# Attention start of a Mamba, mixture-of-experts and attention kernel: first tile gathered in one row, key inputs fetched earlier, keys and ternary pieces redistributed

## The chip, the cores and the metric

The kernel runs on one core of one Trainium2 chip, in one launch. A core has TensorE (PE, with its weight loads shown apart as PEld), VectorE (DVE), ScalarE (ACT), GpSimd (POOL) and SyncE (SP), each with its own instruction queue that is worked off in order, and DMA engines that move data between memory and the core. The metric is the device time of the launch in microseconds (us), as a median of several runs. One more run was recorded with the profiler; all views of the trace are of that run.

## The reference

The input x is [4, 512, 512] (2048 tokens of width 512, 16 tiles of 128 tokens), the context is [4, 512, 256]. Four residual blocks follow each other:

```python
x = x + _L0_xattn_ref(ctx_1024, _layernorm(x, axis=-1), ...)   # selective state-space scan
x = x + _L0_ffn_ref(_layernorm(x, axis=-1), ...)               # 64 experts, top 8, rerouted
x = x + _L1_xattn_ref(_layernorm(x, axis=-1), ctx_1024, ...)   # 16 heads, RMS-normed q and k
x = x + _L1_ffn_ref(x, L1_ffn_w1, L1_ffn_w2)                   # two ternary "bitlinear" layers
```

Three things of it matter here. The experts' results are weighted and added, eight for each token:

```python
y = lax.ragged_dot(hact, jnp.swapaxes(down_proj, 1, 2), group_sizes)
w = top_val.reshape(-1)[order]
out = jnp.zeros_like(x).at[tok].add(y * w[:, None])
```

The attention's keys depend on the context alone, so they can be made at any time before they are read, one task for each of 4 batches and 16 heads:

```python
k = (encoder_hidden_states @ Wk).reshape(B, Skv, H, D)
k = rmsnorm(k, gk)
```

And both weights of the last block are turned into ternary numbers by the mean of their absolute values, which needs two passes over each:

```python
scale = 1.0 / jnp.clip(jnp.mean(jnp.abs(w)), EPS, None)
return jnp.clip(jnp.round(w * scale), -1, 1) / scale
```

## The kernel before

The kernel has stages that follow each other on the same core: the state-space scan (`ssm_phase`, up to about 583 us of the span), the routing (`route`, to about 702), the experts (`Experts.run_in`, to about 1467), a conditional that handles tokens beyond the room of an expert (`tc.If(many > 0)` in `moe_phase`), and the attention with the last feed-forward (`attend`). Inside `ssm_phase`, `route`, `run_in` and `attend` the order of the instructions on each engine is that in which the Python code calls them (`manual_schedule`).

*Keys.* The class `Keys` makes one key at a time in four steps: `task` (two matmuls of PE, pk, L1091), `evict` (ACT squares pk into k_sq and copies it scaled into k_kT, L1100 and L1101, and SP stores k_kT to k_dram), `squares` (PE sums the squares into kpss, L1111) and `take` (ACT takes kpss into k_ms, L1123). Keys are made in three places: beside the scan, in the experts (`key_tasks`, one for each expert until the list is empty) and at the start of the attention (`KEYS_LATE`: heads 8 to 15 of batches 2 and 3, 16 keys). For these last ones two contexts (k_ctx, L2039) and the weights (k_w, L1082) are loaded when the attention begins. `last_keys` turns their mean squares into inverse roots (`rsqrt`, an ACT table load, a square root and five DVE operations), transposes them on PE (pkr, L2092) and stores them to r_dram.

*Experts.* Iteration i of `run_in` gathers the rows and weights of expert i + 2 (POOL's indirect DMAs xg, wg, wd), multiplies gate and up of expert i - 1 (pg, L1191) between the transposes of expert i's rows, runs a key task, and multiplies down for expert i - 2 (po, L1215 and L1225). The rows are stored to y_dram by SP (L1237). Between pg and the next matmuls lie ACT's `sg`, DVE's `h` (L1198, L1200) and ACT's copy of half of `h` (L1202). After each expert a share of a task list is worked off:

```python
while tasks and done < (i - 1) * many / E:
    tasks.pop(0)()
```

The list has 44 tasks that find each token's rows and weights, then the ternary tasks (`Ternary.tasks`: load a piece wf of 1 MB, L1634 and L1636; reduce its absolute values, L1649; a mean over partitions by PE, L1656; and in a second pass scale, clip and round it, L1664 to L1666), then the norms of all earlier keys (`key_norms`: a load of ms_dram, an rsqrt, and PE transposes kpt, L1463).

*Attention's start.* For batch 0 the eight expert rows of each token are gathered from y_dram by POOL (yg, L1132, one 128 x 512 piece for each of 4 tiles x 8 slots, in four buffers) and added into x_all by DVE (L1722). When a tile is complete, its statistics (L1728 on DVE; ve_c, L1732, and rstd_c, L1734, on POOL), its normed form xn_c, its transpose (pt, L1747) and the queries of head groups 0 and 1 (pq, L1790; norms qms and rq on POOL, L1801 and L1802; qn, L1808; transpose pqt, L1817) follow, and the first scores (psc, L1824). All of this is put into a list with due times in an imagined clock, and the list is called in order of these times:

```python
GAP, FLIGHT = 1.25, 3.5
for n in range(NC * TOPK):
    later(n * GAP, fetch, 1)
    later(n * GAP + FLIGHT, add, 1)
...
for i, (b, h) in enumerate(KEYS_LATE):
    later(5 + 2.7 * i, some_keys, b, h)
```

The times set only the order of the calls; an engine that has its inputs does not wait for them. `norm_k` (POOL multiplies kT by its inverse norm rk, L1782) of heads 0 to 2 stands at the times 4, 6 and 8. Before the list, SP is given the loads of k_ctx, k_w, Wq and the first three heads' kT, rk and v.

*Attention's loop.* It runs over units u, four for each of 64 heads: scores for unit u, values (po, L1851) once a head, the transposes (pet, L1844) of unit u - 2, then what `front[u]` and `back[u]` hold. `put` enters work there: queries of the next head group, projections (px, L1860) of the group before, gathers and the feed-forward of earlier batches. In the first four heads no queries and no projections are entered.

Of the kernel before, what the change touches and what calls it, by code (L numbers as in the profile page):

```python
# [731 lines left out]
def moe_phase(ctx, cm, x_all, w, kv, dr, out):  # L732
# [14 lines left out]
    tern = Ternary(cm, keep, w)  # L747
    with ExitStack() as es:
# [3 lines left out]
        with tc.manual_schedule(), tc.tile_pool(name="e_w", bufs=4) as wp:  # L752
            ex = Experts(cm, w, dr, y_dram, r, wp)
            route(cm, x_all, w, kv, dr, r, more, keys, ex)
            ex.run(tern, more, keys, kv)
# [3 lines left out]
    with tc.manual_schedule():  # L759
        attend(cm, x_all, w, kv, y_dram, r["wk"], r["pos"], tern, out)  # L760
# [19 lines left out]
def route(ctx, cm, x_all, w, kv, dr, r, more, keys, ex):  # L780
# [19 lines left out]
    def iota(shape, name, pattern, mult=0, dtype=I32):  # L800
        t = cp.tile(shape, dtype, name=name)
        gp.iota(t, pattern=pattern, base=0, channel_multiplier=mult)
        return t
# [17 lines left out]
    def made(name, shape, pattern, mult=0, dtype=F32):  # L821

        t = iota(shape, f"{name}_i", pattern, mult)
        plan.at(plan.now + 5, cast, t, name, dtype)
# [31 lines left out]
    mT = cp.tile([E, NT, P], F16, name="mT")  # L856
# [383 lines left out]
class Experts:  # L1240
# [18 lines left out]
    def run(self, tern, more, keys, kv):  # L1259
        with ExitStack() as es:  # L1260
            self.run_in(es, tern, more, keys, kv)

    def run_in(self, ctx, tern, more, keys, kv):
# [9 lines left out]
        key_list = key_tasks(keys, self.w, kp, ex.ps)  # L1273
# [3 lines left out]
        done = 0  # L1277
        self.load_rows(0)
        self.load_rows(1)
        for i in range(E + 2):  # L1280
# [10 lines left out]
            if i >= 2:  # L1291
                ends = list(range(ROWS[i - 2], ROWS[i - 1], P)) + [ROWS[i - 1]]
                ex.down(st[i - 2], [self.y_dram[r0:r1, :] for r0, r1 in zip(ends, ends[1:])])
                while tasks and done < (i - 1) * many / E:
                    tasks.pop(0)()
                    done += 1
            keys.squares()
        assert not tasks and not key_list


def key_tasks(keys, w, pool, ps):

    nc = keys.nc
    left = [(1, h) for h in range(3, H)] + [(b, h) for b in (2, 3) for h in (6, 7)]
# [5 lines left out]
    def load(b0, h0, b, h):  # L1310

        if b != b0:
            t = ctx[b] = pool.tile([P, CTX // P, S], F32, name="k_ctx")
            nc.sync.dma_start(t, w["ctxT"][:, b * S:(b + 1) * S].rearrange("(k p) s -> p k s",
                                                                           p=P))
        if h // HG != h0 // HG:
            keys.load(h // HG * HG, (h // HG + 1) * HG, pool, "k_w")

    def task(n):
        keys.task(*left[n])  # L1320
        keys.evict()
        if n + 1 < len(left):
            load(*left[n], *left[n + 1])

    load(-1, -1, *left[0])
    return [lambda n=n: task(n) for n in range(len(left))]
# [290 lines left out]
class Ternary:  # L1617
    def __init__(self, cm, keep, w):
# [4 lines left out]
        self.part = [keep.tile([P, NC], F32, name=f"part{n}") for n in (1, 2)]  # L1623
        self.ws = [keep.tile([P, 1], F32, name=f"ws{n}") for n in (1, 2)]

    def tasks(self, pool, ps):

        cm, nc = self.cm, self.cm.nc

        def load(n, c):  # L1630
            t = pool.tile([P, DH], F32, name="wf")
            src = self.w[f"w{n + 1}T"].rearrange("(c p) o -> c p o", p=P)
            if n == 0:
                nc.sync.dma_start(t, src[c])  # L1634
            else:
                nc.sync.dma_start(t.rearrange("p (k o) -> p k o", k=NC),  # L1636
                                  src[c * NC:(c + 1) * NC].rearrange("k p o -> p k o"))
            return t

        loads = [(n, c) for n in range(2) for _ in range(2) for c in range(NC)]  # L1640
# [6 lines left out]
        def add(n, c):  # L1647
            fetch()
            nc.vector.tensor_reduce(self.part[n][:, c:c + 1], ready.pop(0), AX.X, ALU.add,  # L1649
                                    apply_absolute_value=True)  # L1650

# [8 lines left out]
        def round_(n, c):  # L1660
            fetch()
# [4 lines left out]
            nc.scalar.activation(self.out[n][:, c * DH:(c + 1) * DH], t, AF.Copy, bias=-MAGIC)  # L1666

        nc.vector.tensor_copy(self.identb, cm.ident)
        calls = [(fetch,)]
        for n in range(2):  # L1670
            calls += [(add, n, c) for c in range(NC)] + [(mean, n)]
            calls += [(round_, n, c) for c in range(NC)]
# [14 lines left out]
def attend(ctx, cm, x_all, w, kv, y_dram, wk, pos, tern, out):  # L1687
# [26 lines left out]
    def fetch(n):  # L1714
        for _ in range(n):
            t, k = rows.pop(0)
            ygs.append((gather(nc, pool[4], "yg", DM, y_dram[:, :], pos[:, t, k:k + 1]), t, k))
# [193 lines left out]
    def ffn_up(t, half):  # L1911

        if half == 0:
# [3 lines left out]
            hid = pool[1].tile([P, DH], F32, name="hid", tag="eT" if turn else "hid")  # L1917
# [16 lines left out]
    def ffn_h(t):  # L1934
# [4 lines left out]
        hq = pool[2 if turn else 1].tile([P, DH], BF16, name="hq", tag="qT" if turn else "hq")  # L1939
# [7 lines left out]
    def ffn_hT(t, n):  # L1947
        hid, hq, sc, de = ff[t]
        if n == 0:
            ff["hT"] = pool[1].tile([P, NH, P], BF16, name="Th")  # L1950
# [84 lines left out]
    ctx_k = {}  # L2035

    def load_ctx(b, tag):
        t = ctx_k[b] = pool[1].tile([P, CTX // P, S], F32, name="k_ctx", tag=tag)
        nc.sync.dma_start(t, w["ctxT"][:, b * S:(b + 1) * S].rearrange("(k p) s -> p k s", p=P))  # L2039

    keys = Keys(cm, w, kv, small, lambda n: pool[7].tile([P, S], F32, name=f"k_{n}", tag="oT"),
                lambda shape, name: (pav if name == "kpss" else psc).tile(
                    shape, F32, name=name, tag="po" if name == "kpss" else "psc"),
                lambda b: (ctx_k[b], 0), direct=ms)
    first, end = KEYS_LATE[0][1], KEYS_LATE[-1][1] + 1
    load_ctx(2, "hq")
    keys.load(first, end, pool[1], "hid")
    load_q(0)
    load_ctx(3, "Th")
    load_kv(0)  # L2050
    load_q(1)
    load_kv(1)
    load_kv(2)
# [6 lines left out]
    GAP, FLIGHT = 1.25, 3.5  # L2060
    for n in range(NC * TOPK):
        later(n * GAP, fetch, 1)
# [16 lines left out]
    for n in range(3):  # L2079
        later(4 + 2 * n, norm_k, n)  # L2080
    def some_keys(b, h):
        keys.squares()
        keys.task(b, h)
        keys.take()
        keys.evict()

    def last_keys():
        keys.squares()
        keys.take()
        rsqrt(nc, small, ms, ms, "late")  # L2090
        pr = pav.tile([n_ms, P], F32, name="pkr", tag="po")
# [154 lines left out]
```

## Time and profile before

| | |
|---|---|
| median of 3 runs | 2767.82 us (2764.25 to 2768.01) |
| profiled execution | 2769.29 us, of which the span is 2767.4 us |
| mean granted TensorE clock | 0.948 |
| PE busy | 2539.8 us (92%) in 10107 instructions |
| DVE, ACT, POOL busy | 54%, 46%, 43% |
| DMA | 405.21 MB, mean 146 GB/s |
| chain that ended last | PE 41%, DVE 3%, ACT 1%, DMA 1% of the span |

The span reaches from the first to the last instruction. A matmul's end is modelled in the trace, so a busy PE is not PE at its peak. The clock column gives the part of full TensorE speed that was granted. A view by stretches gives the busy time of each engine in each stretch; the waits view says who waited for whom, in total, how many times and the longest; the timeline lists instructions in order of time, with the idle time before them and what ended it in brackets.

### The profile page before, as it was taken

To read this page: it belongs to the slowest core of one execution; us is meant where nothing else is said; L and a number is where in the kernel's file an instruction comes from. 1 tells how busy PE (TensorE), PEld (TensorE's weight loads), DVE (VectorE), ACT (ScalarE), POOL (GpSimd) and SP (SyncE) were. 2 spreads that over 40 slices of the span, in tenths; PEclk is the share of its full clock that TensorE was granted. 3 is DMA by queue.
4 is the path that set the end of the run, shared out by engine and by line. 5 is a ranking of instruction groups with operands and counts; after the bars stand their busy time and mean duration, and the time that the engine had idled before them with its cause. 6 is when DMAs were issued, how large, how long until landed. Compare 5 with 4: busy or idle time off the path is not lost. (4 is left out here: it accounts for less than half of the span.)

```text
span 2767.4 us, 29904 instructions
## 1 busy us (share of the span) xinstructions
PE 2539.8 (92%) x10107; PEld 1436.0 (52%) x10158; DVE 1486.8 (54%) x2546; ACT 1274.1 (46%) x2363; POOL 1181.3 (43%) x1121
## 2 busy tenths in 40 slices
PE   5989897986899999999985989999999999999997
PEld 2545454653456566666663544445555554555543
DVE  5887877966322223333443365545665666544445
ACT  6675757754323322222332443445555554555543
POOL 4888887961333334443433333224431443121212
PEclk8979797987999999999998999999999999999999
DMA  6253535322656656668986344323332443221200
GB/s 243 81 200 102 200 102 188 119 84 80 195 181 209 209 179 220 222 224 306 343 284 209 122 147 131 95 88 126 114 96 80 126 126 99 80 80 51 64 31 19
DMA packets 198352, 405.21 MB, mean 146 GB/s; under 512 B 30372, under 2 KB 71908, under 8 KB 193073
## 3 DMA queue, kind: packets, MB, share of 16 engines
q1 hardware_dynamic: 155566, 249.86, 26.8%
q0 software_dynamic: 40576, 153.19, 17.4%
q8 instruction: 83, 1.36, 0.2%
q14 instruction: 77, 0.62, 0.1%
q10 hardware_dynamic: 2050, 0.18, 0.1%
HBM read 321.22 MB, written 81.92 MB: 146 GB/s over the span
## 5 line engine op out<-in xcount | busy, mean ns | idle before, releaser
L1827 DVE TENSOR_REDUCE mx<-psc 128x1 f32<-128x512 f32 x256 | 176.5, 690 | 452.5 <-PE psc L1824 446.9
L1191 PE MATMUL pg<-xT,wg 128*128 128x284 f32 (+12 forms) x1536 | 399.9, 404 | 14.2 <-ACT h L1202 12.8
L1191 PEld LDWEIGHTS pg<-xT,wg 128*128 128x128 f32 x1536 | 282.6, 194 | 95.1 <-issue 29.7
L1830 ACT ACTIVATE e<-psc,mx 128x512 f32<-128x512 f32 x256 | 176.0, 687 | 320.4 <-DVE mx L1827 320.0
L488 POOL TENSOR_TENSOR dBu<-bb,du 128x1024 f32<-128x1024 f32 x128 | 299.9, 2367 | 26.8 <-DVE dA L511 19.8
L1132 POOL DMA_INDIRECT xg<-xn_dram,tok x168 | 180.7, 1076 | 209.9 <-PE pt L1175 164.7
L1824 PE MATMUL psc<-kT,qT 128*128 128x512 f32 x512 | 264.0, 597 | 1.6 <-ACT qT L1818 1.6
L1851 PE MATMUL po<-eT,v 128*128 128x512 f32 x512 | 235.0, 602 | 10.3 <-ACT eT L1845 10.2
L1790 PE MATMUL pq<-Wq,xnT 128*128 128x512 f32 x512 | 235.0, 603 | 0.7 <-ACT xnT L1749 0.7
L1860 PE MATMUL px<-Wo,oT 128*128 128x512 f32 x512 | 231.5, 595 | 0.0
L511 DVE TENSOR_TENSOR_SCAN dA<-dA,dBu 128x1024 f32<-128x1024 f32 x80 | 183.1, 2289 | 56.9 <-ACT dA L497 46.4
L1801 POOL TENSOR_SCALAR qms<-qms 128x4 f32<-128x4 f32 x64 | 25.5, 398 | 418.1 <-DVE qms L1799 417.2
L1844 PEld LDWEIGHTS pet<-ident,e 128*128 128x128 f32 x1024 | 126.2, 141 | 147.7 <-issue 124.6
L497 ACT ACTIVATE dA<-delta,negA 128x512 f32<-128x512 f32 x256 | 176.5, 692 | 19.0 <-DVE hc L512 12.6
L470 PE MATMUL pv<-Wv,ctxb 128*128 128x512 f32 x256 | 148.1, 709 | 28.7 <-ACT v L476 28.7
L517 PEld LDWEIGHTS yT<-ident,hc 128*128 128x128 f32 x1024 | 130.1, 153 | 83.1 <-issue 57.9
L1851 PEld LDWEIGHTS po<-eT,v 128*128 128x128 f32 x512 | 97.3, 192 | 139.0 <-issue 117.7
L1132 POOL DMA_INDIRECT yg<-y_dram,pos x128 | 128.9, 1007 | 87.5 <-SPq L757 38.5
L1236 DVE COPY yo<-po 128x512 f32<-128x512 f32 x68 | 47.0, 690 | 219.4 <-PE po L1225 219.3
L1844 PE MATMUL pet<-ident,e 128*128 128x128 f32 x1024 | 154.5, 274 | 6.4 <-DVE e L1836 6.4
L517 PE MATMUL yT<-ident,hc 128*128 128x128 f32 x1024 | 145.3, 293 | 11.1 <-POOL hc L512 6.4
L1836 DVE TENSOR_SCALAR e<-e,tot 128x512 f32<-128x512 f32 x256 | 150.5, 588 | 9.1
(352 smaller groups left out, 4384.6 us busy)
## 6 DMA issues: line engine op xcount, KB each, us to landing
y_dram<-yo SPq DMA_DIRECT2D x110, 256.0 KB
bb<-bc_dram SPq DMA_DIRECT2D x16, 1024.0 KB
cb<-bc_dram SPq DMA_DIRECT2D x16, 1024.0 KB
v_dram<-v SPq DMA_DIRECT2D x64, 256.0 KB
k_dram<-k_kT SPq DMA_DIRECT2D x64, 256.0 KB
Wq<-Wq SPq DMA_DIRECT2D x16, 1024.0 KB
kT<-k_dram SPq DMA_DIRECT2D x64, 256.0 KB
rk<-r_dram SPq DMA_DIRECT2D x64, 256.0 KB
```

The lines of the kernel that those rows point to most:

```text
L488: nc.gpsimd.tensor_tensor(dBus[q], st[b]["bb"][i // 2][:, j:j + 2, :], st[b]["du"][c].unsqueeze(1).to_broadcast([P, 2, S]), ALU.mult)
L497: nc.scalar.activation(dAs[q][:, j, :], st[b]["delta"][c], AF.Exp, scale=negA[:, c, n:n + 1])
L511: nc.vector.tensor_tensor_scan(*flat, 0.0, ALU.mult, ALU.add)
L517: nc.tensor.matmul(yT[:, lc, :], t[:, lc * P:(lc + 1) * P], cm.ident, is_transpose=True, start=first and lc == 0, stop=last, skip_group_ch ...
L1132: nc.gpsimd.indirect_dma_start(out=t[0:n, :], out_offset=None, in_=table, in_offset=bass.IndirectOffsetOnAxis(ap=index, axis=0))
L1191: nc.tensor.matmul(pg[:, 0:n], s["wg"][:, c, m * P:(m + 1) * P], s["xT"][:, c, 0:n], start=c == 0, stop=c == NC - 1)
L1790: nc.tensor.matmul(pq.rearrange("p h d -> p (h d)"), xnTs[b * NC + i][:, c, :], s["Wq"][:, c, :], start=c == 0, stop=c == NC - 1)
L1824: nc.tensor.matmul(pscore, st[b, g]["qT"][:, h, i * P:(i + 1) * P], ks[n], start=True, stop=True)
L1827: nc.vector.tensor_reduce(mx, pscore, AX.X, ALU.max, negate=True)
L1844: nc.tensor.transpose(pt[:, kc, :], e[:, kc * P:(kc + 1) * P], cm.ident)
L1851: nc.tensor.matmul(po, v[:, kc, :], eT[:, kc, :], start=kc == 0, stop=kc == KB - 1)
L1860: nc.tensor.matmul(px, oTs[j * HG + h][:, i * P:(i + 1) * P], st[b, g]["Wo"][:, h, :], start=h == 0, stop=h == HG - 1)
```

## The change

Four things are changed.

1. A pool `late` is opened around the experts and the attention. It holds the tiles named hid, hq and Th, which the attention used for key weights, contexts and the last feed-forward, and in which the routing now also keeps two of its constants. The key tasks of the experts load their inputs there, in a new order (batches 2 and 3 first, then batch 1), with weights for eight heads at a time. After the last of them the context of batch 2 is loaded again, so that contexts and weights of the 16 last keys are in place when the attention begins.
2. The 16 last keys are split: the eight of batch 2 stay in the start (times 0, 2.6, ... 15.6 and 22), the eight of batch 3 are put into the loop, one each head, at the fourth unit of heads 1 to 8. `last_keys` moves into the loop at unit 40.
3. The second four of the first tile's gathers go into a tile yg_first of their own, and `norm_k` and the loads of heads 1 and 2 get later times.
4. Ternary pieces are half as large (4 KB a partition, 512 KB), two loads are asked for ahead, each new load follows the use of a piece, and the whole task list is worked off by the 54th expert.

The diff, cut to these parts:

```diff
@@ moe_phase
+    late = ctx.enter_context(tc.tile_pool(name="b_late", bufs=1))
...
-            ex.run(tern, more, keys, kv)
+            ctx_k = ex.run(tern, more, late, keys, kv)
...
-        attend(cm, x_all, w, kv, y_dram, r["wk"], r["pos"], tern, out)
+        attend(cm, x_all, w, kv, y_dram, r["wk"], r["pos"], tern, late, ctx_k, keys.wk, out)
@@ route
-        t = cp.tile(shape, dtype, name=name)
+        t = late.tile(shape, dtype, name=name, tag="hq") if long else cp.tile(shape, dtype, name=name)
...
-    mT = cp.tile([E, NT, P], F16, name="mT")
+    mT = late.tile([E, NT, P], F16, name="mT", tag="Th")
@@ Experts.run_in
+        QUOTA = 54
...
-                while tasks and done < (i - 1) * many / E:
+                while tasks and done < (i - 1) * many / QUOTA:
@@ key_tasks
-    left = [(1, h) for h in range(3, H)] + [(b, h) for b in (2, 3) for h in (6, 7)]
+    left = [(b, h) for b in (2, 3) for h in (6, 7)] + [(1, h) for h in range(3, H)]
+    late_b = KEYS_LATE[0][0]
...
-            t = ctx[b] = pool.tile([P, CTX // P, S], F32, name="k_ctx")
+            t = ctx[b] = late.tile([P, CTX // P, S], F32, name="k_ctx",
+                                   tag="hq" if b > late_b else "Th")
...
-        if h // HG != h0 // HG:
-            keys.load(h // HG * HG, (h // HG + 1) * HG, pool, "k_w")
+        if h // (2 * HG) != h0 // (2 * HG):
+            h0 = h // (2 * HG) * 2 * HG
+            keys.load(h0, h0 + 2 * HG, late, "hid")
...
+        else:
+            load(*left[n], late_b, KEYS_LATE[0][1])
@@ Ternary.tasks
+        L = NC * DH // (2 * NC)
...
-        loads = [(n, c) for n in range(2) for _ in range(2) for c in range(NC)]
+        loads = [(n, c) for n in range(2) for _ in range(2) for c in range(2 * NC)]
...
         def add(n, c):
-            fetch()
             nc.vector.tensor_reduce(self.part[n][:, c:c + 1], ready.pop(0), AX.X, ALU.add,
                                     apply_absolute_value=True)
+            fetch()
...
         def round_(n, c):
-            fetch()
             t = ready.pop(0)
...
-            nc.scalar.activation(self.out[n][:, c * DH:(c + 1) * DH], t, AF.Copy, bias=-MAGIC)
+            nc.scalar.activation(self.out[n][:, c * L:(c + 1) * L], t, AF.Copy, bias=-MAGIC)
+            fetch()
...
-        calls = [(fetch,)]
+        calls = [(fetch,), (fetch,)]
@@ attend
-    def fetch(n):
+    def fetch(n, into=None):
         for _ in range(n):
             t, k = rows.pop(0)
-            ygs.append((gather(nc, pool[4], "yg", DM, y_dram[:, :], pos[:, t, k:k + 1]), t, k))
+            yg = pool[4].tile([P, DM], F32, name="yg") if into is None else into
+            nc.gpsimd.indirect_dma_start(
+                out=yg, out_offset=None, in_=y_dram[:, :],
+                in_offset=bass.IndirectOffsetOnAxis(ap=pos[:, t, k:k + 1], axis=0))
+            ygs.append((yg, t, k))
...
-    load_ctx(2, "hq")
-    keys.load(first, end, pool[1], "hid")
+    keys.wk = wk_k
+    first = KEYS_LATE[0][1]
     load_q(0)
-    load_ctx(3, "Th")
     load_kv(0)
-    load_q(1)
-    load_kv(1)
-    load_kv(2)
...
+    wide = pool[1].tile([P, KB, S], F32, name="yg_first", tag="eT")
     for n in range(NC * TOPK):
-        later(n * GAP, fetch, 1)
+        later(n * GAP, fetch, 1, wide[:, n - KB] if KB <= n < 2 * KB else None)
...
-    for n in range(3):
-        later(4 + 2 * n, norm_k, n)
+    for f, n, time in ((load_q, 1, 6), (load_kv, 1, 12), (load_kv, 2, 18),
+                       (norm_k, 0, 20.5), (norm_k, 1, 30.5), (norm_k, 2, 40.5)):
+        later(time, f, n)
...
     def some_keys(b, h):
+        keys.task(b, h)
         keys.squares()
-        keys.task(b, h)
+        keys.evict()
         keys.take()
-        keys.evict()
...
-    for i, (b, h) in enumerate(KEYS_LATE):
-        later(5 + 2.7 * i, some_keys, b, h)
-    later(5 + 2.7 * len(KEYS_LATE), last_keys)
+    for i in range(H // 2):
+        later(2.6 * i if i < 7 else 22, some_keys, *KEYS_LATE[i])
+    later(26, keys.squares)
+    later(26.5, keys.take)
...
+    inside[0] = True
+    for i in range(H // 2):
+        u = KB * (i + 1) + 3
+        put(front, u, keys.task, *KEYS_LATE[H // 2 + i])
+        put(back, u, keys.evict)
+        put(front, u + 1, keys.squares)
+        put(back, u + 1, keys.take)
+    put(back, KB * (H // 2 + 1) + 4, last_keys)
```

In the loop the keys take their PSUM from the pool of the queries and projections (pmm) for pk, and k_sq and k_kT lie in the tiles xn_d and Th. The order of the instructions in the built program differs in two further places, at the edges between stages: at the end of the scan DVE's last `yg`, POOL's last sum into x_all and ACT's last key steps stand ahead of the router's first statistics instead of behind them, and at the end of the experts the last copy of `yo` on ACT and its store to y_dram on SP stand behind the branch of the conditional, where before it was the last store of the key norms.

## The prediction

> **What bounds the kernel now.** I read the page first: TensorE (PE) is busy for 92% of the span and the chain that ended last is PE almost everywhere, so time can be won only where PE waits. The busy time by stage, from the windows view, says where that is.
>
> ```profile
> 1300.00:1400.00 100.00, 93.72 (x427) 66.17 (x426) 44.53 (x61) 30.36 (x56) 46.02 (x44) 1.00 0.99 350
> ...
> 1466.00:1511.00 45.00, 17.21 (x61) 8.28 (x57) 10.94 (x16) 7.92 (x17) 18.23 (x18) 0.75 0.76 257
> 1511.00:1578.00 67.00, 64.21 (x242) 35.88 (x242) 29.10 (x48) 27.42 (x58) 33.38 (x38) 0.96 0.40 126
> 1578.00:1601.00 23.00, 14.66 (x39) 7.14 (x38) 8.66 (x20) 8.60 (x17) 7.66 (x9) 0.78 0.51 163
> 1601.00:1634.00 33.00, 30.33 (x104) 14.78 (x105) 22.98 (x44) 17.49 (x41) 7.50 (x7) 1.00 0.47 148
> 1634.00:1760.00 126.00, 122.86 (x395) 60.37 (x394) 78.21 (x142) 50.89 (x116) 46.98 (x49) 0.99 0.39 122
> ```
>
> Columns: stretch, length, busy PE, PEld, DVE, ACT, POOL, granted clock, DMA share, GB/s. The last experts (1300 to 1400) have the DMA engines full. The attention's start holds 1466 to 1511, where PE works 17.2 of 45 us; 1511 to 1578, where it is full; and a gap before the loop at 1601. From 1634 on PE is full. The waits view names the waits: two rows for the experts, three for the start.
>
> ```profile
> PE pg L1191 <- ACT h L1202: 12.8, 4, 5.0
> ...
> PE pm L1656 <- DVE wone L1654: 3.2, 2, 2.3
> ```
>
> ```profile
> PE pk L1091 <- DMA yg<-y_dram,pos: 14.1, 1, 14.1
> ...
> POOL qms L1801 <- DVE qms L1799: 40.9, 6, 9.8
> ...
> POOL kT L1782 <- DMA v<-v_dram: 12.4, 1, 12.4
> ```
>
> The timeline shows the mechanisms.
>
> ```profile
> 1279.40 2.29 DVE L1649 TENSOR_REDUCE part<-wf 128x1 f32<-128x2048 f32 x1 [9.46 <-DMA wf<-w1T]
> ...
> 1282.97 3.75 PE L1191 MATMUL pg<-xT,wg 128*128 128x256 f32 x8 [4.71 <-ACT h L1202]
> ...
> 1489.39 1.27 POOL L1782 TENSOR_TENSOR kT<-kT,rk 128x512 f32<-128x512 f32 x1 [12.38 <-DMA v<-v_dram]
> ...
> 1506.04 0.69 DVE L1728 BATCH_NORM_STATS2 st_c<-x_all 128x6 f32<-128x512 f32 x1
> ...
> 1581.63 0.39 PE L2092 MATMUL pkr<-ident,k_ms 128*64 128x128 f32 x1 [3.52 <-DVE k_ms L100]
> ...
> 1595.67 1.91 PE L1824 MATMUL psc<-kT,qT 128*128 128x512 f32 x2
> ```
>
> A ternary piece that lands late blocks DVE, with it `h`, and PE stands 4.71 us. At the start POOL's fifth gather stands behind a kT*rk product that waits 12.4 us for loads, so tile 0 is complete only at 1506.04. The chain of waits then runs through keys, each costing PE these two pieces:
>
> ```profile
> 1517.28 0.79 PE kpss L1111 x8
> 1518.07 1.84 PE pk L1091 x4
> ```
>
> that is 2.6 us a key.
>
> **Part 1, the experts.** Removed: the late ternary pieces. A 1 MB piece issued at 1270.8 landed at 1279.4. The four waits on `h` are 12.8 us, of which some 12.7 come from these pieces. After the two long ones the next pg took 3.75 instead of 1.89 (half clock), so 3.6 more: 16.3 us won. The pieces of 512 KB are asked for two ahead, so each has about an expert's period (9 to 10 us), and 84 tasks by the 54th expert spread 16 MB over 24 experts instead of 18.
>
> Here a rule speaks against the change. The Trainium skill ("DMA: Bandwidth & Descriptors", section "Bandwidth") wants at least 1 MiB per DMA, and its section "Anatomy of one DMA" fits 2.0 us plus bytes/436e3. An estimate from that is 4.4 us for 1 MiB and 3.2 for 512 KiB, 16 x 2 = 32 us more transfer time in sum. If pieces stood in series on the path, the 16.3 would be gone and more. The row has 8.6 us for a piece with a second beside it; half of it lands in about 4.5, inside the period. I take the row: nothing added.
>
> Added by the order in which the changed program stands. (a) The key norms: the transpose `kpt` now follows its own rsqrt in one expert's tasks (before, an expert later, with no wait). PE waits for ACT's yo copy 0.59, table load 1.28, sqrt 0.36, DVE 1.35+0.36+0.36+0.26+0.36: 5.3 us with hand-overs, and 1.8 for the half clock. Behind it stand all matmuls of the next expert. (b) Each ternary mean follows the last 1.15 us reduction of its own task group: 2 x 2.3 instead of 3.2, +1.4. (c) Two `remap` tasks in one expert: +1. Together 9.5. Net of part 1: -7 us, between -14 (a to c hidden) and +2 (half the old waits stay).
>
> At nothing: the keys' loads inside the experts. They come an expert ahead, at a DMA share of 0.67 to 0.69 in 1000 to 1200. The 1 MB for heads 8 to 15 is the tight one; uncovered it costs 3 us once. On SP a ternary load now waits for ACT's rounding; behind it stand only the next expert's y_dram stores, an expert later. At the edge of the first stage DVE's last `yg` and POOL's last x_all sum move ahead of the router's statistics, and ACT's k_sq ahead of g_xn. The first g_xn comes 3 us later, but PE's first g_pt (590.31) stood behind a kpss that waited 2.95 for k_ms, which now comes sooner: 0, from -1.5 to +1.5.
>
> **Part 2, the attention's start.** Against it: the last y_dram store moves behind the If on SP (ready at 1471.2). With 0.4 to issue and 1.5 (the r_dram store that stood there) to 3.1 us (y_dram before) to land, the first gather goes from 1472.07 to about 1474. For it: eight gathers 1.25 us apart, in four buffers and the four of yg_first, with nothing between; the eighth is issued near 1483 and lands 3.4 us (the first, before) to 6.3 us (the second, beside loads) later. 2 MB of key inputs are off the queue. Statistics of tile 0, after a ninth add, near 1490 instead of 1506.
>
> Then POOL sets the pace: per tile 8 x 1.25, ve and rstd 0.6 to 1.7, two qms/rq pairs 3.0, one kT product 1.27, so 15 to 16 us. Tile 3's statistics fall near 1537 instead of 1563.1, since 8 keys are gone from PE, 21 us, and some of the others done before. From there to the loop's first psc the trace has 32.6 us: two keys 5.2, last_keys' chain 4.0 (1578.15 to 1582.1), a half-clock pq 2.3 (5.90 for 3.60). Without these 21: 1558 instead of 1595.7, -38.
>
> PE will idle some us in each tile. The Trainium skill ("TensorE: Matmul & The Clock Gate", section "What's actually happening") halves the clock after an idle window of about 3.4 us; by it most gaps here stay free, -38. The row after an idle of 3.57 us paid 2.3 for one pq. I take one or two of those on the path: -35, between -26 (6.3 us landings, 19 us a tile) and -40.
>
> SP's order: Wq of group 1 now stands behind three k_dram stores that wait for ACT, issued near 1482 and needed near 1501; the second and third kT/rk/v loads are needed by POOL some 15 us after issue. At nothing; one that is late costs what it is late, up to the 8.6 us of a loaded 1 MB. The kT product of head 0, moved behind the seventeenth gather, is needed only by the first psc, after tile 1's transposes. The rows that share memory through the new pool (Th, hq, hid) are last read by the routing before the experts begin: nothing.
>
> **Part 3, the loop.** Eight keys come into heads 1 to 8, one each: 8 x 2.6 = 20.9. In heads 1 to 3 PE waits 1.3 us a head, mostly for eT behind the scores; a key fills 0.2 of it: -0.6. ACT's 1.45 us a key fits beside the scores. last_keys' transpose waits there for a table load and five small DVE operations, partly under a 3.4 us projection: +2, from 0 to 4. Sum +22, from +17 to +26.
>
> **Sum.** -7 - 35 + 22 = -20 us: from the profiled execution's 2769.3 (span 2767.4 and 1.9 around it) to 2749.3. The median of the runs shown, 2767.82, lies 1.5 lower: 2748.
>
> **Rivals.** *The start saves less than the loop pays* (slower). If gathers and POOL's chain pace tiles 1 to 3 as slowly as before (20 us a tile), the landings stretch to 6 us and the tail keeps half-clock matmuls, the start gives 10, the experts 7 and the loop takes 22: +5, 2773. It decides once the start saves under 15 us. For it: POOL waited 40.9 us for qms. Against: that qms came late because PE did keys, full for 64 of 67 us. Chance 0.07. *The experts give nothing*: new waits (a to c) and late pieces cancel the 16 us, maybe 5 more: 2755 to 2760. For it: DVE's queue is in order and denser in the first 54 experts. Chance 0.15. *More than I take*: `kpt` partly hidden and the start at -40: 2735. Chance 0.08. The forecast itself: 0.70, 2736 to 2760.
>
> **How the numbers follow.** This kernel's measurement can tell about 0.2% (5.5 us) from no change. Forecast 0.70 and the larger gain 0.08 are faster; of the experts' rival 0.10 is faster and 0.05 the same; of the slower one 0.05 slower and 0.02 the same. So 0.88, 0.07, 0.05. The range, 2732 to 2763, takes in both ends of the start and of the experts, not together.
>
> **What would show it.** Right: no wait on `wf` before 1466 and one new PE wait of about 5 us at `kpt`; the first eleven POOL instructions after the If all gathers; tile 0's statistics 14 to 18 us earlier; first psc of the loop 30 to 40 us earlier, counted from the If; then heads 1 to 8 each 2.3 to 2.6 us longer. Wrong: PE waits on pk or pq in the start for loads, a tile period of 19 us or more, or more than 3 us a key in the loop.

## The result and the profile after

The changed kernel takes 2750.22 us (median of 5 runs, 2747.28 to 2757.41) where the kernel before takes 2768.01 (5 runs, 2764.25 to 2776.38) on the same chip; the ratio is 0.9935, interval [0.9916, 0.9955]. That is 17.8 us faster; 20 were forecast. Its profiled execution took 2754.55 us (span 2752.8), 4.3 more than its median; that of before 2769.29, 1.3 more. In the two profiles the gain is thus 14.6 us, and the stage numbers below add up to that.

Four of the stretches that the prediction read in the windows view, now of the changed kernel (stretch, length, busy PE, PEld, DVE, ACT, POOL, granted clock, DMA share, GB/s):

```profile
1300.00:1400.00 100.00, 91.96 (x410) 65.85 (x409) 36.89 (x65) 34.07 (x64) 40.71 (x41) 0.97 0.84 283
...
1466.00:1511.00 45.00, 33.90 (x113) 17.84 (x112) 17.15 (x27) 12.59 (x27) 24.84 (x27) 0.89 0.82 278
1511.00:1578.00 67.00, 52.68 (x151) 27.52 (x152) 34.01 (x58) 20.39 (x42) 33.15 (x38) 0.82 0.37 111
...
1634.00:1760.00 126.00, 122.27 (x408) 62.32 (x407) 67.81 (x135) 54.69 (x120) 39.74 (x43) 0.99 0.41 128
```

The DMA engines of the last experts are no longer full (0.84 instead of 0.99), yet PE is busy for less of that stretch, so something new stands there. The beginning of the start has twice the PE work, 33.9 us instead of 17.2. Its middle, full before, now has PE waiting and the clock at 0.82. The waits view of PE names both, first for the experts (700 to 1466), then for the start (1466 to 1601):

```profile
PE kpt L1475 <- issue: 5.3, 1, 5.3
...
PE pm L1673 <- DVE part L1665: 3.0, 1, 3.0
...
PE pm L1673 <- DVE wone L1671: 2.2, 1, 2.2
...
PE pg L1194 <- ACT h L1205: 0.4, 1, 0.4
```

```profile
PE pqt L1838 <- DVE qn L1829: 12.0, 4, 3.6
PE pk L1094 <- DVE half L1721: 4.6, 1, 4.6
```

The four waits on `h` are gone (12.8 to 0.4) and the forecast ones are there, `kpt` with just the 5.3 us that were worked out, the two means with 5.2 together. The first `pk` waits 4.6 us instead of 14.1. The timeline of the changed kernel gives the marks of the start:

```profile
1474.47 0.95 POOL L1735 DMA_INDIRECT yg<-y_dram,pos  x1 [33.57 <-issue]
...
1492.22 0.69 DVE L1749 BATCH_NORM_STATS2 st_c<-x_all 128x6 f32<-128x512 f32 x1
...
1543.45 0.69 DVE L1749 BATCH_NORM_STATS2 st_c<-x_all 128x6 f32<-128x512 f32 x1
...
1564.91 1.91 PE L1845 MATMUL psc<-kT,qT 128*128 128x512 f32 x2
```

First gather 1474.47 (1474 forecast), tile 0's statistics 1492.22 (1490), tile 3's 1543.45 (1537), the loop's first psc 1564.91 (1558 to 1561). The tiles are 15.4, 18.1 and 17.8 us apart by their statistics, where the sum had 15 to 16.

To read small terms, the span was cut at four marks: the end of the last `pv` of the first stage to the first `g_pt` (edge); the last `plist` matmul, near the end of the routing, to the last PE matmul ahead of the If (experts); from there to the loop's first psc (start); from there to the end (loop). Two profiles of before exist (the second is run e5), two of the changed kernel (the second is e1).

| us | edge | experts | start | loop | span |
|---|---|---|---|---|---|
| before | 7.3 | 766.8 | 128.8 | 1171.7 | 2767.4 |
| before, e5 | 7.3 | 769.1 | 126.8 | 1168.5 | 2767.5 |
| changed | 10.7 | 764.4 | 97.7 | 1187.9 | 2752.8 |
| changed, e1 | 10.9 | 764.6 | 100.2 | 1185.0 | 2755.3 |

The windows view between these marks shows what a stage consists of; first before, then changed, each as experts, start, loop:

```profile
700.02:1466.83 766.81, 734.82 (x3295) 469.37 (x3294) 252.98 (x448) 217.47 (x470) 304.18 (x293) 0.98 0.71 233
1466.83:1595.67 128.84, 90.33 (x322) 49.04 (x322) 45.68 (x77) 40.92 (x84) 55.28 (x61) 0.86 0.54 177
1595.67:2767.40 1171.73, 1137.45 (x4046) 575.51 (x4096) 663.44 (x1434) 562.25 (x1106) 329.66 (x404) 0.99 0.29 91
```

```profile
702.83:1467.25 764.42, 738.43 (x3295) 471.52 (x3294) 256.70 (x471) 219.27 (x478) 294.31 (x293) 0.97 0.71 232
1467.25:1564.91 97.66, 72.66 (x226) 38.74 (x225) 45.79 (x72) 27.24 (x55) 54.02 (x61) 0.85 0.58 190
1564.91:2752.80 1187.89, 1157.88 (x4194) 589.77 (x4193) 658.75 (x1439) 575.81 (x1134) 329.82 (x404) 0.99 0.29 92
```

Length less busy PE is PE's idle time. A second loss hides in the busy time, the half clock: the same view in steps of 5 us (20 in the loop), length times (1 - granted clock), summed, gives it. The remainder is work at full speed. Experts: idle 32.0 to 26.0, clock 18.8 to 20.4, full-speed work 716 to 718. Start: idle 38.5 to 25.0, clock 17.6 to 14.6, work 72.7 to 58.1. Loop: idle 34.3 to 30.0, clock 10.0 to 9.6, work 1127.5 to 1148.3.

### The profile page after: what moved, and what is told of

It reads as the page before. It is cut to its first block, busy times and chain, and to the rows that moved or that the text cites. A ratio compares the mean times of both kernels' runs of the same rounds, so it can differ in the third digit from the quotient of the medians.

```text
span 2752.8 us, 30001 instructions
## 1 busy us (share of the span) xinstructions
PE 2545.1 (92%) x10158; PEld 1441.3 (52%) x10158; DVE 1486.0 (54%) x2570; ACT 1275.9 (46%) x2371; POOL 1170.6 (43%) x1121
## 5 line engine op out<-in xcount | busy, mean ns | idle before, releaser
L1135 POOL DMA_INDIRECT xg<-xn_dram,tok x168 | 172.2, 1025 | 221.6 <-PE pt L1178 179.2
L497 ACT ACTIVATE dA<-delta,negA 128x512 f32<-128x512 f32 x256 | 176.5, 692 | 18.1 <-DVE hc L512 12.0
L1135 POOL DMA_INDIRECT wd<-down,widx x64 | 63.1, 986 | 216.1 <-PE po L1228 182.2
```

Source lines behind the costliest of these rows:

```text
L497: nc.scalar.activation(dAs[q][:, j, :], st[b]["delta"][c], AF.Exp, scale=negA[:, c, n:n + 1])
L1135: nc.gpsimd.indirect_dma_start(out=t[0:n, :], out_offset=None, in_=table, in_offset=bass.IndirectOffsetOnAxis(ap=index, axis=0))
```

## The experiments

**Yardstick.** No edit.

> The changed kernel once more, on the chip and in the rounds of the next three, as their yardstick. Theory: the stage sums of the first profile come back within 1.5 us each: route entered some 2.8 us later than before, experts 2 us shorter, start 31 us shorter, loop 16 us longer; in sum 14 to 18 us faster than the kernel before. Rival: a stage moves by more from run to run than the effects read from it (over 3 us in one stage), and then none of the small terms may be read from a single profile.

2754.03 us (ratio to before 0.993, [0.9916, 0.9945]). The stages stay within 0.2 us in the experts and within 3 us in start and loop, more than the 1.5 expected and just less than the rival's 3; the entry to the route moved by 2.9 because the first stage's own end moved (its last `pv` at 582.5 and 585.2). So marks are counted from the stage's own beginning below. The runs that follow widen the spread: six profiles with the changed kernel's start (the result, e1, e3, e4, e9, e10) show it at 93.8 to 100.2 us, 96.7 in the mean. A difference under 6 us in the start, or under 3 in the loop, is therefore not read from one profile.

The runs were made on several chips. Times of different chips are compared below by what each gains on the kernel before on its own chip; for the changed kernel that is 17.8 us (the result), 16.7 (e1) and 17.8 (e10).

**The kernel before once more.** No edit.

> The kernel before once more, for a second profile to take stages from. Theory (the small stages move from run to run with the half clock): the experts' full-speed work is 716 us within 1 as in the first profile, the waits on h are again 11 to 14 us, and what differs is the time lost to half clock, by up to 6 us in a stage; the loop lies between 1166 and 1173. Rival: the first profile stands for all, every stage within 1 us.

2768.02 us. Full-speed work in the experts is 717.3 (716.0 before), the loop 1168.5. What differs is idle and clock: the start's lost clock is 22.9 instead of 17.6, the loop's 6.2 instead of 10.0. The theory holds, except that the full-speed work moved by 1.3 where 1 was allowed.

**The ternary part alone, in the kernel before.** The class `Ternary` of the changed kernel, and:

```diff
-                while tasks and done < (i - 1) * many / E:
+                while tasks and done < (i - 1) * many / 54:
```

> The kernel before with the ternary part alone: 512 KB pieces, asked for two ahead, tasks spread over 54 experts. Theory (the new waits cancel most of what the late pieces cost): the four waits on h of 12.8 us go to under 1.5 us, a kpt wait of about 5.3 us and two pm waits of 5.2 us in sum appear, and the experts become 2 to 4 us shorter; start and loop stay within 2 us of before; 2764 to 2767 by the median of before. Rival (pieces cost nothing new and the experts' gain is lost elsewhere in the changed kernel, to the key inputs loaded there): experts 8 to 14 us shorter here.

2760.88 us, ratio 0.9967, [0.9954, 0.998], so 5.5 to 12.7 us faster. The waits come as forecast (`h` 0.7, kpt 5.7, the means 5.2). The experts take 761.5 us: 5.3 and 7.6 below the two profiles of before. That lies between the two expectations. All profiles with this part and the old task order, this one included, show the experts at 764.4 to 764.6 or at 761.1 to 761.5, with 20.4 to 20.5 or 17.0 to 17.1 us of lost clock and 26 to 27 of idle: the two groups differ by what is paid in half clock.

**Each TensorE half of a task one expert later.** A task returns its second half, which the next expert runs first:

```diff
+                todo, halves = halves, []
+                for f in todo:
+                    f()
-                while tasks and done < (i - 1) * many / QUOTA:
-                    tasks.pop(0)()
+                while tasks and not halves and done < (i - 1) * many / QUOTA:
+                    half = tasks.pop(0)()
+                    if half:
+                        halves.append(half)
...
         act.copy(wT, pt)
-        pw = ps.tile([P, NC, E], F32, name="pw", tag="pt")
...
+        def rest():
+            pw = ps.tile([P, NC, E], F32, name="pw", tag="pt")
...
+        return rest
```

(so too in `row` and in the ternary `mean`; step 1 of `key_norms` returns an empty half).

> The changed kernel with each task that ends in a TensorE step cut in two, the TensorE half one expert later: the key norms' kpt after rsqrt, the two ternary means (pm), the four remaps (pw), the two rows (prow). The work is the same. Theory: these waits, 5.3 + 5.2 + 3.5 + 2.0 = 16 us in the changed kernel's profile, all go, and with them most of the half clock that follows them (some 15 us lost between 740 and 1466 by the granted clock): experts 20 to 31 us shorter than in the changed kernel, some 2722 to 2732. Rival (the waits only absorb slack: the next expert's gathers or DVE are late anyway): a wait on xg, h or xT takes their place and the experts become under 8 us shorter.

2728.57 us, ratio 0.9846, [0.9834, 0.9859]: 25.5 below e1. The experts take 738.9 us, 22 to 26 less. The waits on pm, pw and prow are gone and kpt waits for nothing; one new wait of 3.3 us came, pt for the copy `krows` behind the second kpt. Idle 13.3 instead of 26.0, lost clock 8.6 instead of 20.4: about half of the gain was never in the list of waits. The experts in the windows view:

```profile
703.35:1442.27 738.92, 725.65 (x3295) 464.47 (x3294) 257.41 (x471) 219.00 (x478) 293.24 (x293) 0.99 0.74 240
```

**The statistics' address.**

```diff
-        sts = self.work.tile([P, 6], F32, name="g_st")
+        sts = self.const.tile([P, 6], F32, name=f"g_st{t % 2}")
```

(so too g_mv, g_ve, g_rstd, g_nmr).

> The changed kernel with the router's statistics tiles (g_st, g_mv, g_ve, g_rstd, g_nmr) taken from the constants' pool instead of the work pool, so that they lie at other addresses and the first statistics wait for no release of the first stage's memory. Theory (the 2.8 us at the edge are an address effect: the new pool shifts the work pool onto memory that the first stage gives up last): the first statistics start near 583 instead of 589.6, the first g_pt near 590 instead of 593.2, and the route ends 2 to 3 us sooner; total 2 to 3 us below the changed kernel. Rival (the order of yg and the last x_all sum costs the 2.8): statistics stay at or after 589.

The timeline of the changed kernel, then of this one:

```profile
589.63 0.70 DVE L158 BATCH_NORM_STATS2 g_st<-x_all 128x6 f32<-128x512 f32 x1 [3.74 <-DMA ms_dram<-k_ms]
...
593.17 1.11 PE L181 MATMUL g_pt<-ident,g_xn 128*128 128x128 f32 x4 [6.14 <-ACT g_xn L174]
```

```profile
582.00 0.68 DVE L159 BATCH_NORM_STATS2 g_st<-x_all 128x6 f32<-128x512 f32 x1
...
590.74 0.72 PEld L182 LDWEIGHTS g_pt<-ident,g_xn 128*128 128x128 f32 x4 [2.67 <-ACT g_xn L175]
```

The edge is 7.1 us; it is 7.3 in both profiles of before and in e2, and in every other run with the new pool and these statistics where the change put them it is 10.4 to 10.9. So the new pool cost 3.4 us at a place that the diff does not touch: by the wait at 589.63, it shifted `g_st` onto memory whose last reader is a store of the first stage. The median, 2754.81, does not resolve it (e1 has 2754.03, and both spread over 11 to 13 us).

**Without the extra row of buffers.**

```diff
-        later(n * GAP, fetch, 1, wide[:, n - KB] if KB <= n < 2 * KB else None)
+        later(n * GAP, fetch, 1)
```

> The changed kernel without the extra row of four buffers: all gathers go through the pool of four again, in the same order. Theory (most of tile 0's 14 us come from the kT product and the key loads that no longer stand among the first gathers): the fifth gather waits for the first add, some 3.5 us, tile 0's statistics come 1 to 4 us later than in the changed kernel, the start is 0 to 4 us longer. Rival (the row of buffers itself gives the gain): statistics over 8 us later, the start 8 to 14 us longer.

2757.42 us. Tile 0's statistics come 31.1 us after the experts (25.0 in both profiles of the changed kernel): 6 us late, between the two. The start takes 100.7, just above the range of 93.8 to 100.2: most of the lateness is made up by tile 3 (79.3 against 76.2 and 78.1). By the medians, though, this run gains 9.5 us on the kernel before on its chip, 7 to 8 less than the changed kernel. The one profile does not show where, so the row of buffers may be worth more than these stages say.

**The kT products back among the gathers.**

```diff
-    for f, n, time in ((load_q, 1, 6), (load_kv, 1, 12), (load_kv, 2, 18),
-                       (norm_k, 0, 20.5), (norm_k, 1, 30.5), (norm_k, 2, 40.5)):
-        later(time, f, n)
+    for n in range(3):
+        later(4 + 2 * n, norm_k, n)
```

with load_q(1), load_kv(1) and load_kv(2) behind load_kv(0).

> The changed kernel with the first three kT products and the loads before them put back where the kernel before has them: Wq of the second group and the second and third kT/rk/v loads asked for at once, the products on POOL behind the fourth, fifth and seventh gather. Keys, early inputs and the row of buffers stay as changed. Theory (the product that waits for its loads among the gathers is the main part of what tile 0 gained): the fifth gather stands 6 to 12 us behind the fourth, tile 0's statistics come 8 to 14 us later than 25 us after the experts, the start is 8 to 15 us longer than the changed kernel's 94 to 100. Rival (the products wait little once the 2 MB of key inputs are off the queue, so it is the early inputs that count): statistics under 5 us later, start under 5 us longer.

2755.11 us. The timeline's POOL and DVE rows:

```profile
1491.63 1.47 POOL L1803 TENSOR_TENSOR kT<-kT,rk 128x512 f32<-128x512 f32 x1 [5.91 <-DMA rk<-r_dram]
...
1502.54 0.69 DVE L1749 BATCH_NORM_STATS2 st_c<-x_all 128x6 f32<-128x512 f32 x1
```

The products wait 7.3 us for loads, tile 0 is 7.9 us late (32.9 after the experts), just under the theory's 8. But the start is 98.5 us, inside the changed kernel's range, and the run gains 14.1 us on the kernel before, not resolved from the changed kernel's 16.7 to 17.8. With eight keys, tile 0's time did not set the start's length.

**All sixteen keys in the start, one every 2.6 us.**

```diff
-    for i in range(H // 2):
-        later(2.6 * i if i < 7 else 22, some_keys, *KEYS_LATE[i])
+    TIMES = [0.0, 2.6, 5.2, 7.8, 10.4, 13.0, 15.6, 18.2, 20.8, 23.4, 26.0, 28.6, 31.2, 33.8, 36.4, 39.0]
+    for i, time in enumerate(TIMES):
+        later(time, some_keys, *KEYS_LATE[i])
```

and no keys in the loop, where `last_keys` thereby moves up to step 8.

> The changed kernel with all sixteen late keys in the start, one every 2.6 us from its beginning as in the kernel before, and none in the loop. Theory: the loop falls back by 15 to 20 us; on TensorE sixteen keys take 42 us from 1472, so tile 0's projections, ready some 30 us after the If, stand behind keys for about 15 us, and the start grows by 12 to 18 us; in sum within 5 us of the changed kernel. Rival (the start's pace is POOL's, the keys fit beside it): start longer by under 6 us, 10 us or more faster than the changed kernel.

2747.57 us, ratio 0.9919, [0.9899, 0.9939]. Start and loop in the windows view:

```profile
1470.45:1570.32 99.87, 86.81 (x322) 48.67 (x321) 45.84 (x72) 37.21 (x79) 54.77 (x61) 0.93 0.63 207
1570.32:2749.40 1179.08, 1139.42 (x4047) 576.70 (x4097) 664.73 (x1439) 565.41 (x1110) 329.67 (x404) 0.99 0.29 91
```

The start holds the eight keys more almost in the time that it has anyway: 99.9 us, inside the range of 93.8 to 100.2, and 3 above its mean. Full-speed work rises by 21.5 us to 79.6, idle falls from 25.0 to 13.1, lost clock from 14.6 to 7.2. My theory of the start fell; the rival's holds there. In sum the kernel gains 19.3 us on the kernel before on its chip, 1.5 to 2.6 more than the changed kernel, which the intervals do not resolve; the rival's 10 us did not come, because the loop is only 6 to 9 us shorter: `pkr`, now early in it, waits 4.5 us for its five small steps, and the loop loses 11.8 us of clock.

**The eight keys in the gaps instead.** TIMES for some_keys: seven every 2.6 us, then 22, 25.5, 30.5 to 60.5 in steps of 5.

> The changed kernel with all sixteen late keys in the start, the second eight one by one between a projection pq and the transposes pqt of its result, where TensorE waits 2.5 to 3.6 us for qn in the changed kernel, and none in the loop. Theory (these waits and the half clock behind them, 25 and 15 us in the start, can hold the keys, whose TensorE work is 14.6 to 21 us): the loop is 15 to 20 us shorter, the start 2 us shorter to 8 longer, in sum 9 to 20 us faster than the changed kernel. Rival (keys in the gaps hold back ACT's squares and the qn chain, so each costs its 2.6): start 18 us or more longer, no gain.

2748.21 us, ratio 0.9934, [0.992, 0.9948]. Start 101.7, within the theory; loop 1177.0, 8 to 11 us shorter and not 15 to 20, for the same `pkr` (4.5) and 12.2 us of lost clock. In sum it gains 18.7 us on the kernel before on its chip, about what the changed kernel gains; the theory's 9 to 20 us did not come. Where in the start the keys stand matters little.

**One piece ahead.**

```diff
-        calls = [(fetch,), (fetch,)]
+        calls = [(fetch,)]
```

> The changed kernel with its 512 KB pieces, each asked for only one ahead (one fetch fewer at the beginning); order and spread of the tasks stay. Theory (two ahead is what cures the late pieces; of two tasks in one expert the second finds its piece just asked for): DVE waits for wf again, PE waits on h for 10 to 40 us in sum, the experts are 8 to 45 us longer than in the changed kernel. Rival (the smaller piece and the spread over 24 experts cure it): waits on h under 3 us, experts within 4 us.

2810.48 us, ratio 1.0153, [1.0138, 1.0169]. The experts take 816.2 us, 52 more. DVE's rows:

```profile
1156.66 1.22 DVE L1665 TENSOR_REDUCE part<-wf 128x1 f32<-128x1024 f32 x1 [7.16 <-DMA wf<-w1T]
...
1179.07 1.22 DVE L1665 TENSOR_REDUCE part<-wf 128x1 f32<-128x1024 f32 x1 [6.30 <-DMA wf<-w1T]
```

A piece that is asked for only behind the use of its predecessor blocks DVE, mostly for 6 to 8 us (13 waits of 1.5 to 10.4 us, 81 in sum), and PE with it. The loss is even above the theory's 45. Without the second piece ahead the gain of the first part is lost: with the smaller pieces and the spread, but one ahead, the whole changed kernel is 42 us slower than the kernel before. Pieces of 1 MB with two ahead, and the spread over 54 experts alone, were not run.

**The key inputs loaded in the start.** The last load of key_tasks was called in attend() instead.

> The changed kernel with the last key inputs (1 MB of ctxT and two pieces of Wk, 2 MB in all) loaded at the beginning of the attention's start instead of in the experts; eight keys in the start and eight in the loop, as in the changed kernel. Theory (early inputs are worth what TensorE waits for at the start, and the start has 25 us of TensorE idle to absorb part of it): the first pk waits for its inputs 12 to 18 us after the experts instead of 4.6, the first gathers share the queues' bandwidth and tile 0's statistics come 1 to 4 us later; start 3 to 10 us longer. Rival (the start is paced by POOL and the gathers, TensorE's early keys are slack): start within 2 us of the changed kernel.

2751.04 us, and no answer: the load kept its place, SP issued it at 993.52 us (992.46 in the changed kernel), although it is written behind the conditional. The run is a third profile of the changed kernel's order (start 93.8, loop 1185.5). What the early inputs alone are worth was not measured by a run.

**All together.** Halves an expert later (each kpt too), statistics' address, sixteen keys in front, and last_keys split:

```diff
+    put(back, KB * 9 + 3, rsqrt, nc, small, ms, ms, "late")
+    put(back, KB * 9 + 6, last_keys)
```

> The changed kernel with what the runs so far point to: every TensorE half of a task an expert later (kpt also spaced from kpt), the router's statistics tiles in the constants' pool, all sixteen late keys in the start one every 2.6 us, and the last keys' rsqrt at the same place of the loop as in the changed kernel with its transpose pkr three steps later. Theory (the effects add): 25 (halves) + 3.4 (edge) + 8 (front keys) + 6 (pkr's wait of 4.5 and its half clock) = 42 us below the changed kernel, 2708 to 2718. Rival (they overlap, the next wait takes over): 2720 to 2730.

2708.01 us (2706.48 to 2709.43), ratio to before 0.978, [0.9767, 0.9794]; 43 us below e10, which has the changed kernel's order and ran on the same chip. The theory had 42.

```profile
703.35:1437.38 734.03, 723.65 (x3294) 463.19 (x3294) 256.55 (x471) 219.23 (x478) 293.98 (x293) 0.99 0.74 242
1437.38:1537.52 100.14, 86.86 (x321) 48.63 (x321) 46.11 (x72) 37.25 (x79) 55.26 (x61) 0.93 0.63 206
1537.52:2706.00 1168.48, 1134.84 (x4047) 575.20 (x4097) 662.97 (x1439) 565.76 (x1110) 330.65 (x404) 0.99 0.29 91
```

Edge 7.1, experts 734.0, start 100.1, loop 1168.5: each effect is there, none took another's place. The loop is back at the 1168.5 to 1171.7 us of before.

## Why the prediction was right, and where its steps were not

The sum was right: -20 forecast, -17.8 by the medians. That it came so close is partly luck, since the largest stage was right for another reason than the one given. By stages over the profiles of the same code in e1 to e12: experts 762.7 on average with the ternary part and the old task order against 768.0 in the two of before, -5.3 (forecast -7); start 97 against 127, -30 (-35); loop 1187 against 1169 (with e2's), +18 (+22); edge +3.4 (0). That makes -14; the profiled executions of the changed kernel were among the slower of their series.

*Experts.* The waits came out as listed: the 12.8 us on `h` removed, kpt and the means near their price. In the mean of the profiles idle time fell by 5.2 us (5.0 by the sum), lost clock by 1.1 (1.8) and full-speed work rose by 1.2 (0). What the sum did not see is where the half clock comes from. I took 3.6 us off for two long waits and added 1.8 for one; in the first pair of profiles lost clock went up, 18.8 to 20.4. It is paid after small gaps too: after the `pw`, which wait 0.7 to 0.9 us, TensorE runs at half speed for a while. Timeline, then windows of 2 us, of the changed kernel:

```profile
881.01 1.10 PE L1418 MATMUL pw<-map,s_wT 64*128 64x64 f32 x8 [0.94 <-ACT yo L1236]
882.96 3.43 PE L1194 MATMUL pg<-xT,wg 128*128 128x300 f32 x8
```

```profile
882.00:884.00 2.00, 2.00 (x14) 1.77 (x13) 0.00 (x0) 0.55 (x2) 0.02 (x1) 0.98 0.79 178
884.00:886.00 2.00, 2.00 (x5) 1.25 (x5) 0.00 (x0) 0.00 (x0) 0.00 (x0) 0.50 1.00 382
886.00:888.00 2.00, 2.00 (x9) 1.63 (x8) 0.00 (x0) 1.00 (x2) 0.00 (x0) 0.67 0.03 7
```

By these rows half clock holds from 884 to about 887.3, so 1.7 us are lost behind a wait of 0.94. Behind the last `pw` it holds twice as long, and 3.2 us are lost in the two stretches:

```profile
920.18 1.10 PE L1418 MATMUL pw<-map,s_wT 64*128 64x64 f32 x8 [0.89 <-ACT yo L1236]
```

```profile
917.83:922.83 5.00, 4.11 (x25) 3.01 (x23) 1.12 (x2) 1.70 (x4) 1.89 (x2) 0.86 0.75 213
922.83:927.83 5.00, 5.00 (x14) 3.69 (x14) 0.00 (x0) 0.59 (x2) 0.00 (x0) 0.50 0.52 189
```

That the task waits bring it is shown by e3: without them lost clock fell from 20.4 to 8.6 us at the same work. The same wait is paid at one time and free at another: `po` waited 1.99 us at 2307.80 in the kernel before and then took 5.40, and waited 1.66 at 2295.82 in the changed kernel and took 3.70.

```profile
2307.80 5.40 PE L1851 MATMUL po<-eT,v 128*128 128x512 f32 x8 [1.99 <-ACT eT L1845]
```

```profile
2295.82 3.70 PE L1872 MATMUL po<-eT,v 128*128 128x512 f32 x8 [1.66 <-ACT eT L1866]
```

*Edge.* I put it at nothing, from -1.5 to +1.5, because I followed the order of `yg` and x_all. In the changed kernel the first statistics wait for a store of the first stage, and with them elsewhere in memory the edge is back at 7.1 us: that wait is the 3.4 us (e4). Reading what the moved instruction waits for would have shown it.

*Start.* The sum came out (-30 of -35), but the step that carried 21 of the 35, "8 keys are gone from PE", is wrong. With all sixteen keys in it the start is 99.9 to 101.7 us (e7, e8, e11), against 97 with eight: the eight cost some 4 us there, not 21. About 27 of the 30 us thus have another cause. PE's waits in the start, of the kernel before and then of e7, which both have sixteen keys there, show what has gone:

```profile
PE pt L1747 <- DVE xn_c L1740: 10.5, 1, 10.5
...
PE pkr L2092 <- DVE k_ms L100: 3.5, 1, 3.5
```

```profile
PE pk L1094 <- DVE half L1721: 4.6, 1, 4.6
PE pqt L1838 <- DVE qn L1829: 3.6, 1, 3.6
PE kpss L1114 <- ACT k_ms L1126: 2.9, 1, 2.9
```

The first `pk` waited 14.1 us before (in e5 14.9, there put down to the load of k_w) and waits 4.6 with its inputs in place. The transpose of tile 0 waited 10.5 us for the late tile (1.4 in e5, where 5.3 us more of clock were lost instead) and does not wait in e7. `pkr`, with its 3.5, has gone into the loop. Idle time fell from 38.5 to 13.1 us and lost clock from 17.6 to 7.2. So early keys and an early tile 0 fill the hole at the beginning that PE had before, whether eight or sixteen keys follow.

Nor does tile 0's time alone set the length: with tile 0 late by 6 and 8 us again, and eight keys, the start is 100.7 and 98.5 us (e6, e12). The only profiles with a start near 127 us are those that have sixteen keys, late inputs and late gathers at once (before, e5, e2). I read this as each side covering for the other: with eight keys TensorE has the slack to catch up for late tiles; with early inputs and early tiles it has the room for sixteen. A stage that two engines share is then as long as the later chain, and I added up what should have been compared. That reading fits all runs, but no run has sixteen keys with only the inputs or only the gathers early, so how the 27 us divide between the two stays open.

*Loop.* A key costs 2.06 us between two psc of a steady head (18.54 instead of 16.48); its work is 2.4 to 2.6. The scores and transposes around it:

```profile
1615.94 1.88 PE L1094 MATMUL pk<-k_ctx,k_w 128*128 128x512 f32 x4
1617.66 1.02 PE L1845 MATMUL psc<-kT,qT 128*128 128x512 f32 x2
...
1622.83 0.95 PE L1114 MATMUL kpss<-ones,k_sq 128*128 128x1 f32 x8
1623.64 1.10 PE L1845 MATMUL psc<-kT,qT 128*128 128x512 f32 x2
```

`pk` costs its 1.72; of `kpss` a part falls into a wait that the head had anyway. Head by head that makes 17.6 for eight keys and 1.7 for last_keys, less what eT and clock waits differed by: about 18 rather than 22. e11 shows that all of it was avoidable, for some 3 us more in the start.

*Piece size.* By the estimate in the prediction, with pieces in series, the rule of the Trainium skill ("DMA: Bandwidth & Descriptors", section "Bandwidth": at least 1 MiB per DMA) would have cost the gain. The fit behind that estimate (its section "Anatomy of one DMA") is given for loads that GpSimd issues, and SP issues these; the row was the right one to take, though its 4.5 us for half a piece were too few: in e9 a piece was used 7.3 us after its issue, still inside an expert's 9 to 10. In these runs the lead decided: with 512 KB two ahead the waits on `h` are 0.4 us instead of 12.8, with 512 KB one ahead the experts take 52 us more. What 1 MB two ahead would do is not known.

*The clock.* The rule of the Trainium skill ("TensorE: Matmul & The Clock Gate", section "What's actually happening"), read as gaps under 3.4 us being free, is not what these traces show: the waits of 0.89 and 0.94 us above were followed by half clock.

## What to carry to other kernels

Count a stage shared by two engines as the later of two chains, not as a sum of savings: eight keys, 21 us of TensorE work, taken off the start paid about 4 us there and cost some 18, with last_keys, in the loop where they went. A task that ends in a TensorE step right behind its own DVE or ACT steps is worth cutting in two, with the second half one round later, even where each wait is only 1 us: in e3 the half clock that went with the waits (11.8 us) was about as much as the idle time (12.7). A new buffer pool can put a distant tile onto memory that is released late (3.4 us here): compare what the first instruction of each stage waits for, not only the order.

## What was not expected of the hardware

- A wait of 0.9 us among small matmuls is followed by some 3 us at half clock (granted clock 0.50 from 884 to 886), once by more than 5 (0.50 from 922.83 to 927.83). Over the experts lost clock came to 20.4 us, of which 8.6 were left without the task waits and 6.8 in the best version.
- Whether a gap of 1.7 to 2.0 us is paid differs from case to case (the two `po` above); experts of the same code took about 761.3 or 764.5 us, and the 3.4 us between them are lost clock (17.0 or 20.4).
- A 512 KB piece took 7.3 us from issue to use in the loaded experts (1149.33 to 1156.66, e9, with a second one issued 0.5 us behind it), not much less than the 8.6 of a 1 MB piece in the kernel before, which also had a second beside it.
